# Layer 1 of a four-layer graph network as one written list of 1,056 steps

## The chip, the cores and the metric

The kernel runs on one core of one Trainium2 chip, as one launch that computes all four layers. The metric is the time of an execution on the device in microseconds (us); lower is better. A core has a matrix engine (TensorE, PE in the profile, with its weight loads shown as PEld), three engines for elementwise work (VectorE = DVE, ScalarE = ACT, GpSimd = POOL), and a queue (SyncE, SP) from which most transfers are issued. Each engine takes its own instructions in its own order and waits on semaphores for the others.

## The reference

The data are `x` of 8 batches x 2,048 nodes x 64 features and a normalised adjacency `adj` of 2,048 x 2,048. Every layer ends in `x = layernorm(x + layer(x))`. Layer 0 is a Chebyshev graph convolution with weights for each node, layer 2 a plain graph convolution, layer 3 a graph convolution with symmetric normalisation. Layer 1, where the change is, attends over 64 hyperedges:

```python
h = x @ W
s = leaky_relu(h @ a_node, 0.2)
alpha = softmax(where(H.T > 0, s, NEG), axis=-1)      # over nodes, per hyperedge
agg = einsum('ben,bnf->bef', alpha, h)
beta = sigmoid((h @ a_gn)[:, None, :] + (agg @ a_ge)[:, :, None])
all_he = elu(beta * h + (1 - beta) * agg)             # per hyperedge and node
industry = einsum('nm,bmf->bnf', adj / deg, x @ W_ind)
he = elu(agg)
attn_scores = lambda f: tanh(f @ fcW + fcb) @ av
coefs1 = softmax(where(H > 0, attn_scores(he), NEG))  # over hyperedges, per node
g = einsum('bne,benf->bnf', coefs1, all_he)
pair = stack([industry, g], axis=2)
coefs2 = softmax(attn_scores(pair), axis=-1)
out = einsum('bnk,bnkf->bnf', coefs2, pair)
```

Layer 2 then needs, for every node, `x @ weight_neighbor` (to be multiplied by the adjacency) and `x @ weight_self`.

## The kernel before

The 2,048 nodes are 16 tiles of 128 nodes (`NT = 16`, `P = 128`); a tile's features for all batches are 512 columns (`BC`). Products with the adjacency are done with a 0/1 mask and a scale for each node, on operands split into a high and a low part (`y_hi`, `y_lo`), so that one tile of such a product is 16 x 2 matmuls of 128x512 that accumulate in one PSUM tile. In the profile they appear as `ind` (industry of layer 1) and `a` (layers 2 and 3); the pool `ps_acc` that they accumulate in has a single buffer, so the first product of a tile waits for the scaled copy (`ind`, on ACT, line 658) of the tile before. The mask of a tile is 1 MB, fetched by SP as `mj_l` (two buffers) or, for tiles 0 and 1 of layer 1, in four parts kept in other tiles' homes (`mp_l`, `mp_l1b`).

For every tile j, layer 1 does three things.

- **unit** (`units`, from line 776): `sx` (scores by matmul), `ST` and `tau` (ACT), `gates` (DVE); then, in two halves i = 0, 1 of at most four hyperedges of a node: `ch` (POOL, gate times h), `gp` (PE, gather), `m` and `z` (DVE), `exp` (ACT), `e` (DVE), `w` (POOL); `dp` (PE) and `t3` (ACT) for nodes with more; `a0`, `ga` (POOL sums), `red` (PE), `g` (DVE).
- **product** (`industry`, from line 646): step `i` is a part of the 32 matmuls of industry, step `ind` the scaled copy.
- **mixer** (`mix_and_norm`, from line 917): `dlt` (DVE, industry minus g), `xg` (the kept x is fetched by SP, POOL adds g), `tr`, `sT`, `fc` twice (transpose on PE, copy on ACT, matmul on PE, once for g and once for industry), `th0`, `th1` (ACT, tanh), `sub` (DVE), `df` (PE, line 960: the scores, with `av` repeated in 32 columns and the four blocks in the four column groups of the PE array), `rw` (ACT), `rt` (PE), `sw` (ACT), `mult`, `r`, `s`, `centre` (DVE), `sq` (ACT), `var` (DVE), `rstd` (POOL, two instructions), `x2` (ACT, eight instructions).

`gp` and `exp` use the PSUM pool `ps_g` (one buffer), `fc` the pool `ps_fc` (one buffer), `sx` and `df` the pool `ps_s` (one buffer), and `dp`, `red` and all transposes the pool `ps_m` (two buffers).

The order is written out by hand. Inside `program_order()` (line 213) every instruction of PE, DVE, ACT and POOL is tied to the one before it on its engine, so that the order of the calls is the order on each engine. First comes a head (lines 682 to 757) for the hyperedges' own scores: `agg`, `he`, a transpose, `fche`, the tanh `the`, the scores `sep` (line 723: eight products with one column each), `ese`, then the sums `dnp` for all 16 tiles (line 737). In it six of the 16 steps of tile 1's product are done. Then come the string `ramp` (tiles 0 and 1), the string `turns`, repeated for t = 1 to 14, where turn t works on the unit of tile t + 1 (its `sx` on t + 2), the product of tile t + 1, the mixer's first part of tile t - 1, its second part of tile t - 2 and its end of tile t - 3; and four strings `ending`. A tile's product is eight steps `i` of four matmuls in a turn.

Layer 2's own projections (`features2`, `layer2`, lines 1009 to 1039: a transpose `tr` and the copy `xT`, sixteen small matmuls `u`, then `y_hi` on ACT and two DVE instructions) stand in the strings `ending` as `K` and `L`, that is, after turn 14; K takes its PSUM from `ps_fc`, L from `ps_g`. The first tile of layer 2's product is the step `A` there, two matmuls each. After the list, POOL adds layer 2's bias to the 16 tiles `x2` (line 1127), and layers 2 and 3 run as loops over tiles (from line 1894); their first fetched mask, `mj_l` of tile 1, uses memory that layer 1 gives up.

Of the kernel before, what the change touches and what calls it, by code (L numbers as in the profile page):

```python
# [9 lines left out]
F32 = mybir.dt.float32  # L10
# [53 lines left out]
def kernel(  # L64
# [547 lines left out]
    def layer1(  # L612
# [25 lines left out]
        homes = {"g": (0, 1, 2, 3), "dlt": (4, 5, 7), "ind": (14, 15), "r": (8, 9, 10),  # L638
# [7 lines left out]
        def industry(j):  # L646

            if j == 0:
                acc = early[1]
            else:  # L650
                a = second if j == 1 else mask_tile(mjp, j, "l1")
                acc = ps_acc.tile([P, BC], F32, tag="acc", name=f"ind_{j}")
                for mt in range(NT):
                    times_mask(acc, a, i_hi, i_lo, mt)
                    if mt % 2 == 1 or j == 1:
                        yield "i"
            ind = row("ind", f"ind_{j}")
            nc.scalar.activation(ind, acc, AF.Copy, scale=cols_of["sdeg"][:, j:j + 1])
            ind_of[j] = ind
            yield "ind"  # L660

        g_of, ind_of, dlt_of = {}, {}, {}
        product = {j: industry(j) for j in range(NT)}
        second = mask_parts(own, 1, (7, 8, 9, 12), "l1b")

        def ahead(n):
            for _ in range(n):
                assert next(product[1]) == "i"

        with tc.tile_pool(name="fa", bufs=2) as fa:  # L670
# [10 lines left out]
            with program_order():  # L681
                agg = fa.tile([P, BC], F32, tag="hs", name="agg", bufs=3)
                nc.vector.tensor_tensor(b_view(agg), b_view(aggp), bcast(rden), ALU.mult)

                he = fa.tile([P, BC], F32, tag="xT", name="he")
                nc.scalar.activation(he, agg, AF.Exp, bias=minus1)
                low = slice(64, P)

# [5 lines left out]
                nc.vector.scalar_tensor_tensor(he, he, 1.0, agg, op0=ALU.min, op1=ALU.max)  # L694
                sums = fa.tile([P, 2, B], F32, tag="sums", name="sums", bufs=1)
                late = [own.tile([P, NT - NE, 2, B], F32, tag="b0_11", name="rest_sums")]
                early[0](NT)
                assert next(product[0]) == "ind"
                tr = ps_tr.tile([P, NP, P], F32, tag="tr", name="trhe")
                for pr in range(NP):  # L700
                    transpose(tr[:, pr, :], he[:, pr * P:(pr + 1) * P])
                heT = fa.tile([P, NP * P], F32, tag="hs", name="heT", bufs=3)
                nc.scalar.copy(heT, tr.rearrange("p r c -> p (r c)"))
                parts(agg1, agg)
                ahead(1)
                fc = ps_mm.tile([P, 2, QW], F32, tag="mm", name="fche")
                for h in range(2):
                    rs = slice(h * 64, (h + 1) * 64)
                    nc.tensor.matmul(fc[:, h, :], fcw_sb[rs], heT[rs], start=True, stop=True)
                th = fa.tile([P, 2, QW], F32, tag="the", name="the", bufs=1)  # L710
                nc.scalar.activation(th, fc, AF.Tanh, bias=fcg_sb)
                nc.vector.scalar_tensor_tensor(
                    b_view(he), b_view(agg), -1.0,
                    vecs[:, 2, :].unsqueeze(1).to_broadcast([P, B, C]), op0=ALU.add, op1=ALU.mult,
                )
                nc.vector.tensor_reduce(sums[:, 0, :], b_view(he), AX.X, ALU.add)
                full = fa.tile([P, BC], F32, tag="full", name="full", bufs=1)
                nc.vector.tensor_scalar(full, agg, -1.0, None, op0=ALU.mult)
                parts(nagg, full)
                ahead(3)  # L720
                sp = ps_tr.tile([P, QW], F32, tag="sm", name="sep")
                for b in range(B):
                    nc.tensor.matmul(
                        sp[:, b:b + 1], th[:, b % 2, (b // 2) * P:(b // 2 + 1) * P], av_sb,
                        start=True, stop=True,
                    )
                ahead(2)
                ese = fa.tile([P, B], F32, tag="ese", name="ese", bufs=1)
                nc.vector.tensor_scalar(ese, sp[:, 0:B], TOP, None, op0=ALU.min)
                nc.scalar.activation(ese, ese, AF.Exp)  # L730
                ese2 = fa.tile([P, 2, B], F32, tag="ese2", name="ese2", bufs=1)
                nc.vector.tensor_copy(r_(ese2[:, 0, :]), ese)
                nc.vector.tensor_tensor(r_(ese2[:, 1, :]), ese, ese2[:, 0, :], ALU.subtract)

                def weight_sums(dn, lo, hi):
                    for j in range(lo, hi):
                        nc.tensor.matmul(
                            dn[:, j - lo].rearrange("p k b -> p (k b)"),
                            r_(pT[0:E, j * P:(j + 1) * P]),
                            r_(ese2[0:E].rearrange("p k b -> p (k b)")), start=True, stop=True,  # L740
                        )
# [5 lines left out]

                dn = ps_tr.tile([P, NT, 2, B], F32, tag="tr", name="dnp")
                weight_sums(dn, 0, NE)
                nc.vector.tensor_copy(sums[:, 1, :], ese)  # L750
                parts(ext, sums)
                rec = fa.tile([P, NE, B], F32, tag="rec", name="rec", bufs=1)
                nc.scalar.copy(rec, dn[:, 0:NE, 0, :])
                reciprocals(rec, dn[:, 0:NE, 1, :], 0, NE)
                dn2 = ps_mm.tile([P, NT - NE, 2, B], F32, tag="mm", name="dnp2")
                weight_sums(dn2, NE, NT)
                nc.scalar.copy(late[0], dn2)
# [5 lines left out]
        mjp = stack.enter_context(tc.tile_pool(name="mj1", bufs=2))  # L763
# [153 lines left out]
        def mix_and_norm(j):  # L917

            ind, g = ind_of[j], g_of[j]
            dlt = row("dlt", f"dlt_{j}")
            nc.vector.tensor_tensor(dlt, ind, g, ALU.subtract)
            yield "dlt"
            xr = row("xr", f"xr_{j}")
            nc.sync.dma_start(xr, kept[j])
            r = row("r", f"r1_{j}")
            nc.gpsimd.tensor_tensor(r, g, xr, ALU.add)
            yield "xg"  # L930

            th = wts.tile([P, 2, BC], F32, tag="pm", name=f"th_{j}")
            fcs = []
            for i, src in enumerate((g, ind)):
                mv = ps_m.tile([P, BC], F32, tag="m", name=f"trm_{j}_{i}")
                for pr in range(NP):
                    pc = slice(pr * P, (pr + 1) * P)
                    transpose(mv[:, pc], src[:, pc])
                yield f"tr{i}"
                sT = small("sT", f"sT_{j}_{i}", (P, BC))  # L940
                nc.scalar.copy(sT, mv)
                yield f"sT{i}"
                if i == 1:
                    nc.scalar.activation(th, fcs[0], AF.Tanh, bias=fcg_sb)
                    yield "th0"
                fc = ps_fc.tile([P, 2, BC], F32, tag="fc", name=f"fc_{j}_{i}")
                for h in range(2):
                    rs = slice(h * 64, (h + 1) * 64)
                    nc.tensor.matmul(fc[:, h, :], fcw_sb[rs], sT[rs], start=True, stop=True)  # L949
                fcs.append(fc)  # L950
                yield f"fc{i}"
            nc.scalar.activation(fc, fc, AF.Tanh, bias=fcb_sb)
            yield "th1"
            nc.vector.tensor_tensor(th, fc, th, ALU.subtract)
            yield "sub"
            df = ps_s.tile([P, QW], F32, tag="sm", name=f"df_{j}")
            for half in range(2):
                for h in range(2):
                    k = 2 * half + h
                    nc.tensor.matmul(  # L960
                        df[32 * k:32 * k + 32, 0:2 * P], av32,
                        th[:, h, half * 2 * P:(half + 1) * 2 * P],
                        start=True, stop=True, tile_position=(0, 32 * k),
                    )
            yield "df"
            rows = small("rows", f"rows_{j}", (P, 2 * P), 1)
            nc.scalar.activation(rows, df[:, 0:2 * P], AF.Tanh, scale=0.5)
            yield "rw"
# [48 lines left out]
        def layer2(j):  # L1017
# [21 lines left out]
            )  # L1039

        unit = {j: units(j, g_of) for j in range(NT)}
# [1483 lines left out]
```

## Time and profile before

| | us |
|---|---|
| median of 3 runs | 1240.49 |
| lowest, highest | 1237.93, 1248.48 |
| profiled execution, time | 1245.25 |
| profiled execution, span | 1243.8 |
| start of the first `sx` of tile 0 | 676.42 |
| start of turn 2, of turn 14 (its first `gp`) | 718.09, 903.52 |
| first product of layer 2's tile 1 | 980.11 |

The profile is of one execution, 1.45 us of whose time lie outside its span. It gives the busy time of each engine, the span in 40 slices of 31 us with the granted clock of TensorE in tenths of full speed (9 stands for 0.9 and more), the chain of work that ended last, and groups of instructions by line, with the shape of their operands, their count, busy time and mean. A stretch can be asked for by its times: then the answer holds busy time of each engine, the clock as a fraction, and the share of the DMA engines. "x8" after a group means eight instructions. A matmul's busy time includes its drain, so that successive matmuls overlap: 32 of them at 0.39 us each take 7.4 us.

### The profile page before, as it was taken

To read this page: it belongs to the slowest core of one execution; us is meant where nothing else is said; L and a number is where in the kernel's file an instruction comes from. 1 tells how busy PE (TensorE), PEld (TensorE's weight loads), DVE (VectorE), ACT (ScalarE), POOL (GpSimd) and SP (SyncE) were. 2 spreads that over 40 slices of the span, in tenths; PEclk is the share of its full clock that TensorE was granted. 3 is DMA by queue.
4 is the path that set the end of the run, shared out by engine and by line. 5 is a ranking of instruction groups with operands and counts; after the bars stand their busy time and mean duration, and the time that the engine had idled before them with its cause. 6 is when DMAs were issued, how large, how long until landed. Compare 5 with 4: busy or idle time off the path is not lost.

```text
span 1243.8 us, 19792 instructions
## 1 busy us (share of the span) xinstructions
PE 1201.1 (97%) x7476; PEld 960.9 (77%) x7476; DVE 886.8 (71%) x1670; ACT 391.3 (31%) x1019; POOL 506.6 (41%) x429
## 2 busy tenths in 40 slices
PE   9999899999999999999999899999988999999996
PEld 7877688888888888888887566666656788888885
DVE  4556578888888888888785778888865656565454
ACT  3100102222222222222233567777765411111111
POOL 2000572555555555555312778888861700000000
PEclk9999999999999999999998799999997999999998
DMA  8987833333333333332454222222200333334551
GB/s 291 240 242 202 202 112 111 106 113 106 108 109 113 107 108 106 107 111 94 161 163 152 76 102 102 102 102 94 93 26 1 136 105 133 107 130 161 178 174 66
DMA packets 101416, 157.11 MB, mean 126 GB/s; under 512 B 12992, under 2 KB 64320, under 8 KB 95552
## 3 DMA queue, kind: packets, MB, share of 16 engines
q1 hardware_dynamic: 96512, 151.38, 37.6%
q10 hardware_dynamic: 4368, 4.33, 1.0%
q8 instruction: 61, 1.00, 0.3%
q0 software_dynamic: 432, 0.05, 0.1%
q14 instruction: 43, 0.35, 0.1%
HBM read 117.97 MB, written 37.76 MB: 125 GB/s over the span
## 4 chain that ended last, share of the span: by engine, by line
PE 87%; DVE 4%; DMA 3%; ACT 3%; issue 2%; POOL 1%; SPq 0%; DVEq 0%; ACTq 0%; POOLq 0%
PE pp L1321 26%; PE a L1782 18%; PE ind L1782 9%; PE y2p L1278 9%; PE y1p L569 6%; PE fc L949 3%; DMA adj<-in_at 2%; PE yp L1881 1%; PE gp L851 1%; PE trm L168 1%; PE try L168 1%; PE dp L869 1%; PE hp L1446 1%; PE u L1027 1%; PE red L900 1%
## 5 line engine op out<-in xcount | busy, mean ns | idle before, releaser
L1332 DVE SCALAR_TENSOR_TENSOR r<-pp,emb_sb,r 128x256 f32<-128x256 f32 x512 | 247.4, 483 | 79.0 <-PE pp L1321 64.9
L1321 PE MATMUL pp<-w_sb,y2T 64*128 64x256 f32 x1024 | 154.2, 378 | 3.3 <-DVE y2T L1294 3.3
L1321 PE MATMUL pp<-w_sb,xT 64*128 64x256 f32 x1024 | 155.9, 381 | 0.6 <-DVE r L1332 0.6
L1321 PE MATMUL pp<-w_sb,y1T 64*128 64x256 f32 x1024 | 153.8, 377 | 0.0
L1190 POOL TENSOR_TENSOR ms<-msk,srow 128x1024 f32<-128x1024 f32 x30 | 76.6, 2552 | 95.3 <-DVE msk L449 95.3
L1321 PEld LDWEIGHTS pp<-w_sb,y2T 64*128 64x128 f32 x1024 | 99.8, 188 | 15.0 <-DVE y2T L1294 3.7
L1321 PEld LDWEIGHTS pp<-w_sb,y1T 64*128 64x128 f32 x1024 | 99.6, 188 | 11.4
L1321 PEld LDWEIGHTS pp<-w_sb,xT 64*128 64x128 f32 x1024 | 95.5, 187 | 13.1 <-issue 2.8
L569 PE MATMUL y1p<-x_hi,m 128*128 128x512 f32 x256 | 102.9, 402 | 0.0
L569 PE MATMUL y1p<-x_lo,m 128*128 128x512 f32 x256 | 100.5, 393 | 0.0
L1782 PE MATMUL a<-v_hi,mj_l 128*128 128x512 f32 x256 | 100.1, 392 | 0.0
L1782 PE MATMUL a<-v_lo,mj_l 128*128 128x512 f32 x256 | 100.0, 391 | 0.0
L1782 PE MATMUL a<-y_hi,mj_l 128*128 128x512 f32 x240 | 96.0, 400 | 2.1 <-DMA mj_l<-mask 2.1
L1782 PE MATMUL a<-y_lo,mj_l 128*128 128x512 f32 x240 | 95.9, 400 | 0.0
L1782 PE MATMUL ind<-y_hi,mj_l 128*128 128x512 f32 x224 | 95.4, 426 | 0.0
L1278 PE MATMUL y2p<-y_hi,msk 128*128 128x512 f32 x240 | 94.7, 395 | 0.0
L1278 PE MATMUL y2p<-y_lo,msk 128*128 128x512 f32 x240 | 93.5, 390 | 0.0
L1782 PE MATMUL ind<-y_lo,mj_l 128*128 128x512 f32 x224 | 88.4, 395 | 0.0
L886 POOL TENSOR_TENSOR ez<-ez,coef 128x1024 f32<-128x1024 f32 x32 | 69.8, 2183 | 37.9 <-DVE ez L881 37.9
L1230 DVE SCALAR_TENSOR_TENSOR ms<-ms,adj 128x1024 f32<-128x1024 f32 x30 | 67.2, 2242 | 0.0
L1513 POOL TENSOR_TENSOR hs<-h,es 128x512 f32<-128x512 f32 x15 | 15.6, 1043 | 116.2 <-ACT hgr L1485 116.2
L1782 PEld LDWEIGHTS ind<-y_hi,mj_l 128*128 128x128 f32 x224 | 42.2, 188 | 20.8 <-issue 12.8
(332 smaller groups left out, 2431.9 us busy)
## 6 DMA issues: line engine op xcount, KB each, us to landing
mj_l<-mask SPq DMA_DIRECT2D x45, 1024.0 KB, 4.9
adj<-in_at SPq DMA_DIRECT2D x64, 256.0 KB, 3.8
mask<-msk SPq DMA_DIRECT2D x32, 512.0 KB, 4.5
raw<-in_at SPq DMA_DIRECT2D x31, 512.0 KB, 5.9
oh<-oh SPq DMA_DIRECT2D x32, 128.0 KB, 3.7
xT<-in_xt SPq DMA_DIRECT2D x16, 256.0 KB, 3.2
xs<-in_xn SPq DMA_DIRECT2D x16, 256.0 KB, 2.7
kept<-x SPq DMA_DIRECT2D x16, 256.0 KB, 3.6
```

Source lines behind the costliest of these rows:

```text
L168: nc.tensor.matmul(dst, src, ident, start=True, stop=True, is_transpose=True)
L569: nc.tensor.matmul(accs[q][jj], r_(m[:, t, jj * P:(jj + 1) * P]), r_(part[:, mt, :]), start=i + h + t == 0 and part is x_hi, stop=i == 3 a ...
L851: nc.tensor.matmul(gp[:, u, :], r_(t["oh"][:, 2 * i + u, :]), r_(agg1), start=True, stop=True)
L886: nc.gpsimd.tensor_tensor(by_b(ezs[i]), by_b(ezs[i]), per_b(t["coef"], 2 * i, 2), ALU.mult)
L949: nc.tensor.matmul(fc[:, h, :], fcw_sb[rs], sT[rs], start=True, stop=True)
L1190: nc.gpsimd.tensor_tensor(ms, m, srow[j].unsqueeze(1).to_broadcast([P, 8, P]), ALU.mult)
L1230: nc.vector.scalar_tensor_tensor(ms, ms, 1.0, raws[j][h], op0=ALU.mult, op1=ALU.not_equal, accum_out=bad[:, 2 * j + h:2 * j + h + 1],)
L1278: nc.tensor.matmul(acc, r_(msk[j, mt // 8][:, mt % 8, :]), r_(part[:, mt, :]), start=mt == 0 and part is y_hi, stop=mt == NT - 1 and part ...
L1321: nc.tensor.matmul(pp[:, h, pl, :], terms[j][name][rs, 2 * bq + pl], w_sb[rs, k, dq * 4 * C:(dq + 1) * 4 * C], start=k == 0, stop=k == K - 1,)
L1332: nc.vector.scalar_tensor_tensor(rb, ppv[:, :, dd, :], emb_sb[:, j, d:d + 1], rb, op0=ALU.mult, op1=ALU.add)
L1513: nc.gpsimd.tensor_tensor(b_view(hs), b_view(h_sb[:, j, :]), bcast(es[:, j, :]), ALU.mult)
L1782: nc.tensor.matmul(acc, r_(a[:, mt, :]), r_(part[:, mt, :]), start=mt == 0 and part is hi, stop=mt == NT - 1 and part is lo,)
```

## The change

The change rewrites layer 1's order.

- Every step of a tile becomes a function that can be called alone (`industry`, `units`, `mixer`, `layer2`), and one list of tokens "tile.step" says the order: 33 tokens in the head, 1,023 behind it. `perform` calls them one by one. The strings `ramp`, `turns` and `ending` are gone.
- The steps are no longer in turns. Typically the unit of tile j runs with the product of tile j or j - 1 and the mixers of tiles j - 2 and j - 3. Step `i` is always four matmuls, and the 115 of them behind the head stand one at a time between other steps. Five stand in the head (ten of tile 1's sixteen pairs, six before).
- The masks of tiles 1 to 4 are asked for at the start of layer 1: 1 and 2 in four parts each in homes of other tiles, 3 and 4 in the pool `mj1`, which is opened earlier. From tile 5 on a mask is asked for when the product two tiles before has ended (before: likewise, with the pool opened after the head). The loads of `pT` stand behind these masks on SP and wait for memory of layer 0's last tile; before, they stood ahead of it.
- `xr` of tiles 0 and 1 is fetched at the start of the list and that of tile j + 2 at `xg` of tile j.
- Layer 2's projections are six steps (`f`, `xT`, `mm`, `hi`, `add`, `lo` are their tokens), which begin right after the last product of layer 1 and stand between the steps of tiles 14 and 15. `mm` alternates between `ps_g` and `ps_fc`, except where tile 15's `fc` holds the latter. The sixteen steps `A` stand among them from tile 5's `lo` on.
- The hyperedges' scores `sep` take the form of `df`: four products with `av32` as weights in column groups, a copy of 128x256 by DVE, two transposes, and a view of the result (before: eight products with the tanh as weights and `av` as the only column).
- `dlt` is a `scalar_tensor_tensor` instead of a `tensor_tensor`. Industry has a third home (11).

```diff
-        homes = {"g": (0, 1, 2, 3), "dlt": (4, 5, 7), "ind": (14, 15), "r": (8, 9, 10),
+        homes = {"g": (0, 1, 2, 3), "dlt": (4, 5, 7), "ind": (14, 15, 11), "r": (8, 9, 10),
...
-        second = mask_parts(own, 1, (7, 8, 9, 12), "l1b")
...
+            def products():
+                if j == 0:
+                    early[0](NT)
+                    acc_of[j] = early[1]
+                    return
...
+                for mt in range(done_of[j], done_of[j] + 2):
+                    times_mask(acc_of[j], mask_of[j], i_hi, i_lo, mt)
+                done_of[j] += 2
...
+        at_home = {1: (7, 8, 9, 12), 2: (2, 3, 5, 10)}
+        mjp = stack.enter_context(tc.tile_pool(name="mj1", bufs=2))
...
+        def by_columns(dst, th):
+            for half in range(2):
+                for h in range(2):
+                    k = 2 * half + h
+                    nc.tensor.matmul(
+                        dst[32 * k:32 * k + 32, 0:2 * P], av32,
+                        th[:, h, half * 2 * P:(half + 1) * 2 * P],
+                        start=True, stop=True, tile_position=(0, 32 * k),
+                    )
...
+        head = (
+            "1.mask 2.mask 3.mask 4.mask c.agg 0.i c.hexp c.he 0.ind c.trhe c.agg1 c.heT "
+            "c.fche c.sums c.the c.nagg 1.i c.sep 1.i c.serow c.sert 1.i c.ese c.eexp c.ese2 "
+            "c.dnp c.ext 1.i c.rec c.hgr c.dnp2 1.i c.late "
+        )
...
-                for b in range(B):
-                    nc.tensor.matmul(
-                        sp[:, b:b + 1], th[:, b % 2, (b // 2) * P:(b // 2 + 1) * P], av_sb,
-                        start=True, stop=True,
-                    )
...
-            nc.vector.tensor_tensor(dlt, ind, g, ALU.subtract)
...
+                nc.vector.scalar_tensor_tensor(
+                    t["dlt"], ind_of[j], 1.0, g_of[j], op0=ALU.mult, op1=ALU.subtract
+                )
...
+                    "0.xr 1.xr c.rests 0.sx 0.dp 0.ST 0.gates 0.gp0 0.tau 1.sx 0.ch0 0.m0 0.gp1 1.ST "
+                    "1.dp 1.gates 0.m1 0.ch1 1.tau 2.sx 0.z0 1.i 1.ch0 0.t3 2.gates 1.i 0.exp0 0.z1 "
+                    "1.i 2.tau 0.e0 0.exp1 1.gp0 1.ch1 2.ST 0.e1 1.ind 2.i 0.w0 1.t3 1.m0 1.gp1 2.i "
+                    "1.z0 0.w1 2.i 0.a0 1.exp0 2.i 1.m1 0.ga 1.e0 0.red 3.sx 1.z1 2.ch0 2.gp0 3.ST "
+                    "2.dp 0.g 1.exp1 2.m0 1.w0 0.tr0 2.i 0.sT0 1.e1 0.tr1 2.i 2.z0 0.xg 2.xr 0.sT1 "
+                    "0.fc0 0.dlt 2.exp0 1.a0 3.gates 2.i 0.th0 1.w1 2.e0 2.i 3.tau 0.fc1 2.ind 2.ch1 "
+                    "2.gp1 0.th1 3.i 2.m1 2.w0 2.t3 0.sub 1.red 4.sx 1.ga 2.z1 3.dp 4.ST 4.gates 2.a0 "
...
+                    "9.i 8.sT1 8.dlt 11.tau 7.df 10.gp0 8.th0 9.w1 9.i 10.m0 7.rw 8.fc1 6.x2 10.z0 "
+                    "7.rt 10.ch1 9.i 10.exp0 9.ga 9.red 9.i 10.t3 10.e0 9.i 9.g 11.ch0 8.th1 10.gp1 "
+                    "9.i 7.sw 10.m1 10.w0 7.mult 12.sx 10.z1 9.i 11.mask 12.ST 9.tr0 7.r 9.ind 9.xg "
...
+                    "15.dlt 0.mm/g 1.xT 15.th0 2.f 0.add 3.f 0.hi 1.mm/f 2.xT 0.lo 4.f 1.hi 1.add "
+                    "2.mm/g 3.xT 1.lo 5.f 2.hi 2.add 3.mm/f 4.xT 2.lo 6.f 3.hi 3.add 4.mm/g 5.xT 3.lo "
+                    "15.tr1 4.hi 4.add 5.mm/f 15.sT1 4.lo 14.rt 5.hi 5.add 7.f 6.xT 0.A 5.lo 14.sw "
+                    "6.mm/g 14.mult 14.r 8.f 6.hi 6.add 15.fc1 7.xT 6.lo 9.f 14.s 15.th1 7.mm/g "
+                    "14.centre 8.xT 15.sub 1.A 7.hi 10.f 9.xT 2.A 7.add 14.sq 15.df 7.lo 8.mm/f 15.rw "
...
+                    "10.mm/f 11.xT 15.r 14.x2 9.lo 12.f 13.f 15.s 3.A 9.add 10.hi 4.A 15.centre "
+                    "11.mm/g 12.xT 10.lo 15.sq 10.add 14.f 11.hi 5.A 15.var 13.xT 12.mm/f 11.lo "
+                    "15.rstd 11.add 6.A 12.hi 12.add 13.mm/g 14.xT 12.lo 15.x2 7.A 13.add 14.mm/f 8.A "
+                    "13.hi 14.add 15.f 14.hi 13.lo 9.A 15.xT 14.lo 10.A 15.mm/g 11.A 15.hi 15.add "
+                    "12.A 15.lo 13.A 14.A 15.A "
```

## The prediction

> **What bounds the kernel now.** I read the slices first, then the chain of waits with its shares, then the chain in order of time through layer 1, then busy times by stretch.
>
> ```profile
> PE   9999899999999999999999899999988999999996
> PEclk9999999999999999999998799999997999999998
> PE 87%; DVE 4%; DMA 3%; ACT 3%; issue 2%; POOL 1%; SPq 0%; DVEq 0%; ACTq 0%; POOLq 0%
> ```
>
> PE bounds nearly everything: 87% of the chain. Its weak slices are 22 to 23 and 30 to 31, the start and the end of layer 1. Three stretches, first the ramp (tile 0's `sx` to turn 2), then one turn, then the end:
>
> ```profile
> 676.42:718.09 41.67, 37.10 (x130) 25.05 (x131) 28.20 (x50) 19.21 (x52) 29.55 (x19) 0.76 0.25 89
> 718.09:733.54 15.45, 15.45 (x76) 10.16 (x75) 12.88 (x20) 9.45 (x22) 10.74 (x8) 1.00 0.28 102
> 918.90:980.11 61.21, 49.30 (x408) 35.84 (x407) 35.51 (x55) 35.11 (x81) 21.14 (x19) 0.89 0.08 28
> ```
>
> Columns: stretch and length, busy time of PE, PEld, DVE, ACT, POOL, granted clock, DMA share, GB/s. In a turn PE is busy throughout at clock 1.00; nothing is to be had there. In the ramp and the end it is idle, and the clock is at 0.76 and 0.89. So the change can gain where PE waits, and lose wherever it makes PE wait in the 13 full turns.
>
> The price of each step on PE comes from the chain in one turn (start, length, group):
>
> ```profile
> 731.47 2.07 PE ind L1782 x8
> 733.54 0.46 PE gp L851 x2
> ...
> 735.47 1.06 PE fc L949 x4
> 736.53 0.59 PE trm L168 x4
> 737.12 0.86 PE dp L869 x2
> ...
> 744.57 0.86 PE red L900 x2
> 745.42 0.93 PE ind L1782 x4
> 746.35 0.57 PE df L960 x8
> ```
>
> So `i` (four matmuls) costs 0.93, `gp` 0.46 and 0.66, `fc` 1.06, `red` 0.86, `dp` 0.86 + 0.23, `tr` 0.44 and 0.59, `sx` 0.81, `rt` 0.22, and `df` 0.57 and 0.21 more that the products behind it lose (2.07 for eight, elsewhere in the turn 1.86). Of the end, at clock 1.00: `f` 0.58, `mm` 1.10 (16 matmuls `u`), `A` 0.46. On the others, from the groups by form: DVE 1.22 for the 1,024-column steps `m0`, `z`, `e`, `sub`, 0.70 for `m1`, 0.68 for 512 columns, 0.81 for `gates`; ACT 1.12 for `exp`, `th`, 1.75 for `t3`, 2.03 for `x2`, about 0.6 for 512 columns; POOL 1.91 and 1.04 for `ch`, 2.2 for `w`, 1.29 for `a0`, `ga`, `xg`, 1.92 for `rstd`. A tile's sums are PE 15.5, DVE 13.6, POOL 13.1, ACT 12.2.
>
> **What the list's work costs.** PE's price of the 1,023 steps behind the head is 269.7 (7.8 + 0.2 per tile for unit and mixer, 115 `i`, and 16 times `f`, `mm`, `A`: 34.3). The same work lay between 676.42 and 980.11, that is 303.7, with 1.9 more (two `i` now stand in the head). 32 us are lost in ramp and end.
>
> **Head.** Up to `fche` (667.22) nothing moves. Then PE: `sep` took 1.68 and is now priced like `df`, 0.57; added are DVE's copy of 128x256 (nearest rows: 0.39 for ACT's `rows`, half of 0.68 for a DVE copy of 512: 0.35) and two transposes (0.22). An `i` stands after each, so the longer chain from the tanh's end (669.58) runs: `sep` 670.2, copy 670.7, `rt` behind an `i` 671.4, `ese`, exponential and split (0.75 in the trace) 672.3; four `dnp`, `i`, twelve `dnp`, `i`. The sixteen took 3.31, which I leave. First `sx`: 677.0 instead of 676.42, bounds 676 and 678, with 1.9 more done. On SP `pT` now stands behind masks 1 to 4 and, by the waits in the built program, needs the memory of layer 0's last tile, free after the last `aggp` (663.1), where it went out at 629.4; by the row of `pT` (7.0 us to landing) and eight issues of 0.44 its last piece is there at about 673, where the last `dnp` needs it at 675: hidden, worth up to 2 us if not. `oh` of tile 0 follows at 667 and lands 4.6 later, before 677. 3 MB of masks land under layer 0's last tile; the early part of mask 0 queues behind one of them (4.9), from 632 to 640, and is needed at 646.
>
> **Ramp.** I walked the list with those durations from 677.0, giving each step the later of its engine's turn and its operands. PE does 5.73 of `sx`, `dp`, `gp` of tiles 0 to 2 and three `i` while tile 0 goes `gates`, `tau`, `ch0`, `z0`, `exp0`, `e0`; the second `gp0` needs `e0` (`ps_g` has one buffer) and waits 1.6. The first product of tile 2 needs `ind` of tile 1, which stands on ACT behind `exp1` and `ST`: 0.6. POOL has most work in the next stretch (16.9 against PE's 15.1) but started ahead. Tile 3's first product comes at 703.8: 24.1 of price and 2.7 idle. Before, 26.8 of price took 41.67. Clock: in the trace it fell to 0.50 during the sixteen `dnp`, after a stretch (664 to 666) with PE busy for 0.52 of 2 us and then matmuls of 1 and 16 columns; here 512-column products stand among them, and I price at full clock. At 0.76, as before, the ramp costs 7 more.
>
> **Middle and end.** From there to the last `A` PE's price is 245.6. Summed from one tile's first product to the next one's, PE is the largest everywhere but in two sections (tile 7: DVE 18.8 against 17.8; tile 12: 13.7 against 13.4): +1.4. What remains is waiting inside a section. Below: 0, as in 13 turns. Above: 18, what the end lost before. In one loop that I followed (tiles 9 and 10), `gp1` waits for `gp0`, `m0`, `z0`, `exp0`, `e0`: 4.8 plus semaphores 0.3, against 5.9 of PE work between; `fc1` has 0.5 to spare. Margins are of the size of one small step, so some are missed: 0.6 per tile, 8, nearer to the turns' row because every resource is the turns'. In the end, two buffers for `mm` give 1.10 + 0.59 + 0.69 + 0.69 and 0.2 of semaphores, 3.3 for two tiles, just under PE's 3.4; before, one buffer at a time left PE waiting for `y_lo`:
>
> ```profile
> 928.58 0.69 DVE x L1036
> 929.27 0.60 DVE y_lo L1037
> ...
> 975.22 4.76 DMA mj_l<-mask
> ```
>
> Tile 15's chain from `df` to `f` is 9.8 against 13.0 of PE work in between. The last line is layer 2's next mask, waited for 2.3 us by PE. It now waits for tile 15's `rstd`, behind which `x2`, `f`, `xT`, `mm`, `hi`, `lo`, `A` still take 6.3: hidden; 4.9 if these are quicker. Uninterrupted products also spare layer 2's first 4 us at clock 0.5 to 0.6: 1.2.
>
> **Sum.** 703.8 + 245.6 + 1.4 + 8 = 958.8 instead of 980.11, and 1.2: **-22.5 us**. Against the profiled execution (span 1243.8, time 1245.25) that is 1222.7; it lies 4.8 above the median, so against 1240.49 I predict 1218.0. Without waits 1208.6; with 18 of them 1228.
>
> `dlt` as `scalar_tensor_tensor`: 0.684 for both forms in the turns. But one `dlt` took 1.66, while POOL's sum ran, whose successor then took 1.72 instead of 1.29:
>
> ```profile
> 703.34 1.66 DVE L924 TENSOR_TENSOR dlt<-ind,g 128x512 f32<-128x512 f32 x1
> ```
>
> The `scalar_tensor_tensor` rows with two operands in SBUF never exceed 0.69, POOL's `w` beside them goes from 1.90 to 2.28. I take 0 on DVE, and 2.2 for `w` holds the rest. The Trainium skill, "SBUF — State Buffer", section "Who interferes with whom", says that a VectorE instruction with two SBUF inputs and a GpSimd one that reads SBUF exclude each other for a whole instruction. It speaks against the change, which gives up turns where they rarely meet: were four such steps of each tile blocked by 1 us, DVE would need 17.6 of 15.5 and the sum be +11 instead of -22.5. The trace has one such wait in 16 `dlt`, so I weigh it low.
>
> **Rivals.**
> - *The margins are missed*: the list is in order on every engine, so one late step (a POOL sum, `ind` behind `exp` on ACT) delays the next. DVE at 88% and POOL at 85% of a tile speak for it, their idle 2 us per turn against. At 2.3 per tile instead of 0.6 the gain is gone: 1236 to 1245.
> - *The clock*, slower than before: between 922 and 934 PE was busy for 7.86 of 12 us and was then granted 0.50 until 938; `u` took 2.01 instead of 1.09. The old turns held 1.00 by running products of 8 and 12; single `i` between waiting steps may not. Half clock for a time T costs T/2. It decides once PE idles by a third, 5 us in a tile: from 70 us of it on (4 or 5 tiles) the result is slower by over 1%, 1253 to 1265. The skill's "TensorE: Matmul & The Clock Gate", section "A second HAM failure mode: psum-queue depth-cycling", describes such small pauses; the turns' 1.00 stands against it.
> - *The change does only half of what it says*: layer 2's projections in the gaps lengthen tiles 14 and 15 (`fc` shares `ps_fc` with `mm`), and the end loses its 18 as before: 1228.
>
> **Chances.** Forecast 0.60 (1208 to 1225), half 0.10 (1225 to 1231), margins missed 0.17 (1228 to 1250), clock 0.13. A measurement of this kernel tells 1% from nothing: faster by over 1% 0.68, within 1% 0.19, slower 0.13. The range goes from 1206 (no waits, a quicker head) to 1242, with the slowest cases outside.
>
> **What would show it.** First `sx` near 677; tile 3's first product near 704 at clock near 1.0; some 15.5 per tile; layer 2's tile 1 at 957 to 962 with no wait for a mask; layers 2 and 3 unchanged in length. Sections longer than PE's price with idle named by DVE or POOL prove the first rival, clock under 0.9 between 704 and 950 the second.

## The result, and the profile after

The changed kernel takes **1228.35 us** (median of 4 executions, 1225.07 to 1229.4), the kernel before, run beside it, 1242.3 (4, 1237.93 to 1248.48): a ratio of **0.988, interval 0.983 to 0.993**. In a second comparison it was 1230.92 (10 executions) against 1239.97 (17), ratio 0.993, interval 0.991 to 0.996; one more execution of the kernel before ran at a mean granted clock of 0.84 instead of 0.98, took 1354.88 and is not counted. So the changed kernel is faster, by some 9 to 14 us and not by the 22.5 forecast.

The profiled execution has a span of 1227.7 and a time of 1229.4; its span is 16.1 shorter than that of before. The slices and the chain's shares of the page, after:

```profile
PE   9999899999999999999999999999999999999996
...
PEclk9999999999999999999998999999999999999998
...
PE 73%; DVE 13%; DMA 4%; issue 3%; ACT 3%; POOL 2%; SPq 0%; DVEq 0%; ACTq 0%; POOLq 0%
```

Both weak spots of PE's row (slices 22 to 23, 30 to 31) are filled, and the clock is granted in full but for slice 22 and the last. Yet PE holds 73% of the chain where it held 87%, and DVE 13% instead of 4%: TensorE shows as busy nearly everywhere, but what sets the end has moved in part to VectorE. The busy times by stretch (columns as in the prediction) tell where. In order: the ramp, one section of the middle (from tile 10's first product to tile 11's), the end (last product of layer 1 to the first of layer 2's tile 1), and all that follows:

```profile
677.59:703.33 25.74, 24.27 (x113) 16.40 (x112) 22.52 (x43) 15.81 (x43) 20.11 (x13) 1.00 0.14 41
...
832.14:848.77 16.63, 14.28 (x70) 9.15 (x67) 15.46 (x29) 10.78 (x31) 11.36 (x8) 1.00 0.24 86
927.90:966.41 38.51, 38.43 (x379) 29.40 (x378) 28.31 (x44) 26.53 (x59) 11.70 (x11) 1.00 0.18 70
966.41:1227.70 261.29, 251.31 (x1185) 205.16 (x1183) 148.58 (x240) 40.60 (x81) 13.39 (x10) 0.99 0.38 131
```

Ramp and end are as hoped: PE busy for 24.3 of 25.7 and 38.4 of 38.5, clock 1.00. The middle isn't: PE works 14.3 of 16.6 in that section, DVE 15.5. The list's DVE work there is 13.7 by the prices of the prediction, and `gates` of one more tile, 0.8, fell into it. The rest is steps that took longer than their price, and four groups say which (smallest, median and largest duration in ns):

```profile
L1008 DVE SCALAR_TENSOR_TENSOR dlt<-ind,g x16: 672/729/2146, 699.0 to 929.0; 128x512 f32<-128x512 f32 x16
L1071 DVE SCALAR_TENSOR_TENSOR dlt<-sw,dlt x16: 677/688/2442, 710.5 to 950.8; 128x512 f32<-128x512 f32 x16
L1076 DVE SCALAR_TENSOR_TENSOR r<-dlt,r x16: 674/691/2277, 713.8 to 951.6; 128x512 f32<-128x512 f32 x16
L1086 DVE SCALAR_TENSOR_TENSOR r<-s,r x16: 678/1374/2082, 716.2 to 954.0; 128x512 f32<-128x512 f32 x16
```

These are `dlt`, `mult`, `r` and `centre`. The same four in the kernel before:

```profile
L924 DVE TENSOR_TENSOR dlt<-ind,g x16: 679/684/1662, 703.3 to 941.6; 128x512 f32<-128x512 f32 x16
L979 DVE SCALAR_TENSOR_TENSOR dlt<-sw,dlt x16: 680/684/685, 721.7 to 962.0; 128x512 f32<-128x512 f32 x16
L983 DVE SCALAR_TENSOR_TENSOR r<-dlt,r x16: 679/681/693, 723.5 to 962.8; 128x512 f32<-128x512 f32 x16
L988 DVE SCALAR_TENSOR_TENSOR r<-s,r x16: 679/681/693, 730.9 to 966.4; 128x512 f32<-128x512 f32 x16
```

There none but `dlt` exceeded 0.693. Summed over the 64 instructions, what goes beyond each line's fastest is 4.8, 7.7, 7.4 and 10.8: **30.7 us** (before: 1.4, 0.1, 0.1, 0.1). Apart from one step of tile 0 (`a0`), they alone of DVE's large steps here have both operands in SBUF; `z`, `e`, `sub` and `g`, which read one from PSUM, stay within 3% of their shortest.

The timeline (start, duration, engine, line, operation; rows of VectorE and GpSimd alone) shows a collision in the changed kernel:

```profile
891.85 0.68 DVE L1071 SCALAR_TENSOR_TENSOR dlt<-sw,dlt 128x512 f32<-128x512 f32 x1
892.08 2.22 POOL L971 TENSOR_TENSOR ez<-ez,coef 128x1024 f32<-128x1024 f32 x1 [0.35 <-DVE ez L966]
892.57 2.28 DVE L1076 SCALAR_TENSOR_TENSOR r<-dlt,r 128x512 f32<-128x512 f32 x1
894.26 2.35 POOL L925 TENSOR_TENSOR d<-h,sig 128x1024 f32<-128x1024 f32 x1
```

GpSimd's `w` starts while `mult` runs and is lengthened from 1.90 to 2.22. Then `r` starts while `w` has 1.73 left and takes 2.28, which is 0.68 and 1.60 more: it waits until `w` is nearly over. The next GpSimd step, `ch`, starts inside `r` and is lengthened in turn. Over the 57 instructions of these lines between 700 and 932, the excess is the rest of the GpSimd step under way less 0.13 in nearly every case (the longest, 2.44, came when a step had 0.04 left and then waited for the whole of the next one). The exception is GpSimd's `rstd` (the power of 128x8): DVE steps that started beside it took 0.68 to 0.69. That is how the old turns escaped, as the timeline of the kernel before shows:

```profile
735.88 1.67 POOL L1000 TENSOR_TENSOR rstd<-var,mhalf 128x8 f32<-128x8 f32 x1
736.51 0.69 DVE L924 TENSOR_TENSOR dlt<-ind,g 128x512 f32<-128x512 f32 x1
...
737.11 0.69 DVE L979 SCALAR_TENSOR_TENSOR dlt<-sw,dlt 128x512 f32<-128x512 f32 x1
...
746.33 0.68 DVE L988 SCALAR_TENSOR_TENSOR r<-s,r 128x512 f32<-128x512 f32 x1
746.50 2.28 POOL L886 TENSOR_TENSOR ez<-ez,coef 128x1024 f32<-128x1024 f32 x1 [0.64 <-DVE ez L881]
```

`dlt` and `mult` stand beside `rstd`, and `r` and `centre` start about 0.2 ahead of a `w`, so that GpSimd waits and not VectorE. Thirteen turns had this same layout; in the list it comes only now and then.

### The profile page after: what moved, and what is told of

It reads as the page before. It is cut to its first block, busy times and chain, and to the rows that moved or that the text cites. A ratio compares the mean times of both kernels' runs of the same rounds, so it can differ in the third digit from the quotient of the medians.

```text
span 1227.7 us, 19772 instructions
## 1 busy us (share of the span) xinstructions
PE 1187.7 (97%) x7470; PEld 942.0 (77%) x7470; DVE 911.2 (74%) x1671; ACT 388.8 (32%) x1019; POOL 512.4 (42%) x429
## 3 DMA queue, kind: packets, MB, share of 16 engines
q1 hardware_dynamic: 96944, 151.38, 38.4%
## 4 chain that ended last, share of the span: by engine, by line
PE 73%; DVE 13%; DMA 4%; issue 3%; ACT 3%; POOL 2%; SPq 0%; DVEq 0%; ACTq 0%; POOLq 0%
PE pp L1457 26%; PE a L1918 19%; PE y2p L1414 9%; PE y1p L569 5%; PE ind L1918 3%; DMA xraw<-in_xn 2%; DVE d L947 2%; DVE ez L966 1%; DVE gp L944 1%; PE u L1146 1%; DMA adj<-in_at 1%; PE yp L2017 1%; PE try L168 1%; DVE r L1086 1%; PE hp L1582 1%
## 5 line engine op out<-in xcount | busy, mean ns | idle before, releaser
L1918 PE MATMUL ind<-y_hi,mj_l 128*128 128x512 f32 x208 | 91.2, 438 | 0.1
L1918 PE MATMUL ind<-y_lo,mj_l 128*128 128x512 f32 x208 | 81.9, 394 | 0.0
L971 POOL TENSOR_TENSOR ez<-ez,coef 128x1024 f32<-128x1024 f32 x32 | 65.2, 2039 | 12.8 <-DVE ez L966 12.7
L925 POOL TENSOR_TENSOR d<-h,sig 128x1024 f32<-128x1024 f32 (+1 forms) x32 | 50.1, 1569 | 32.6 <-ACT sig L903 18.3
```

The source lines that it names most:

```text
L925: nc.gpsimd.tensor_tensor(d[:, 0:n].rearrange("p u (b c) -> p u b c", b=B), b_view(h_sb[:, j, :]).unsqueeze(1).to_broadcast([P, n, B, C]), ...
L971: nc.gpsimd.tensor_tensor(by_b(ezs[i]), by_b(ezs[i]), per_b(t["coef"], 2 * i, 2), ALU.mult)
L1918: nc.tensor.matmul(acc, r_(a[:, mt, :]), r_(part[:, mt, :]), start=mt == 0 and part is hi, stop=mt == NT - 1 and part is lo,)
```

## The experiments

Two theories. **Collisions**: these four steps and GpSimd's steps hold each other up, DVE is late for TensorE's next operand, and this is the missing gain. **Order**: the list's margins are missed anyhow, and the long DVE steps fill idle time. A third, named in the first expectation, is that other traffic slows these steps. "The stretch" is that from tile 3's first product to layer 2's tile 1: 703.33 to 966.41 in the changed kernel, 263.1 (263.2 in its second profile).

### Four steps with one operand in SBUF

```diff
-                nc.vector.scalar_tensor_tensor(
-                    t["dlt"], ind_of[j], 1.0, g_of[j], op0=ALU.mult, op1=ALU.subtract
-                )
+                nc.vector.tensor_reduce(t["dlt"][:, 0:B], b_view(ind_of[j]), AX.X, ALU.add)
...
-                nc.vector.scalar_tensor_tensor(
-                    t["r"], t["dlt"], 0.5, t["r"], op0=ALU.mult, op1=ALU.add
-                )
+                nc.vector.tensor_reduce(t["dlt"][:, 0:B], b_view(t["r"]), AX.X, ALU.add)
```

and likewise `mult` (a sum over `sw`) and `centre` (a sum over `s`). Such a kernel computes something else; it is run for its time alone.

> Leaves out the arithmetic of four VectorE steps of each tile of layer 1 (dlt, mult, r, centre): each becomes a sum over 512 columns with one operand in SBUF, in the same place and behind the same waits, of the same length (the sums s and var take 0.67 to 0.69 in every profile here). The output is therefore not the layer's. Theory 'collisions' (a VectorE step with two operands in SBUF and a GpSimd step hold each other up, which cost these four lines 30.7 us beyond their 0.68 in the changed kernel): all 64 take 0.66 to 0.70, VectorE's busy time between the first sx and layer 2's tile 1 falls from 278 to 246 to 250, the stretch from tile 3's first product to layer 2's tile 1 falls from 263.1 to 250 to 255, the time by 8 to 13 against the changed kernel's 1228. Rival 'order' (the list's margins are missed whatever VectorE does): the lines shorten, but the stretch stays at 260 to 264 and the time within 3 of 1228. Rival 'other traffic' (the long steps are slowed by TensorE, ScalarE or transfers): the sums are stretched as well, up to 2 us.

It took 1206.99 (ratio to the kernel before 0.977, interval 0.971 to 0.982). All four lines were at 0.67 to 0.69, so no other traffic slows them:

```profile
L1008 DVE TENSOR_REDUCE dlt<-ind x16: 673/677/690, 695.7 to 906.8; 128x8 f32<-128x512 f32 x16
L1068 DVE TENSOR_REDUCE dlt<-sw x16: 674/677/687, 707.3 to 928.5; 128x8 f32<-128x512 f32 x16
L1071 DVE TENSOR_REDUCE dlt<-r x16: 674/685/687, 709.0 to 929.3; 128x8 f32<-128x512 f32 x16
L1078 DVE TENSOR_REDUCE r<-s x16: 675/680/686, 711.5 to 931.7; 128x8 f32<-128x512 f32 x16
```

The stretch fell to 944.11 - 700.09 = **244.0**, by 19.1, more than the 8 to 13 expected. Between first `sx` and layer 2's tile 1 DVE's busy time is 224.8 instead of 254.3 (these are the rows by stretch, which count overlapping instructions once; with each counted in full it is 274 and 245, not the 278 and 246 to 250 of the expectation). PE's idle is gone, here in the section of tile 10 again, in the one after it, and in the end:

```profile
832.66:847.84 15.18, 15.18 (x76) 9.56 (x75) 11.31 (x13) 11.15 (x28) 13.06 (x10) 1.00 0.23 82
818.86:832.66 13.80, 13.80 (x70) 9.49 (x68) 12.34 (x22) 10.41 (x32) 9.07 (x8) 1.00 0.35 121
905.60:944.11 38.51, 38.45 (x378) 29.46 (x377) 28.27 (x44) 26.21 (x58) 11.69 (x11) 1.00 0.18 69
```

Tile 10's section is 13.80, all of it TensorE, instead of 16.63. The end is 38.51 in both kernels: all 19.1 came from the middle. With the collisions away TensorE is idle for 0.06 us of the whole stretch, where it was for 13.8 in the changed kernel; "order" has nothing left to explain.

### The same edit in the kernel before

> The kernel before, with the same four steps (dlt, mult, r, centre) turned into sums with one operand in SBUF; their arithmetic is left out. Theory 'collisions': the old turns had hardly any (1.4 us in all, dlt and mult beside rstd, r and centre started just ahead of a GpSimd step that waited for them), so nothing is to be had: the turns stay at 15.45 and the time within 0.5% of the kernel before, where the same edit took 21 us off the changed kernel. GpSimd's w beside r and centre shortens from 2.2 to 1.9. Rival: the sums are cheaper for another reason than the second operand (fewer bytes written, a wait that went with dlt), and the kernel before gains 8 us or more as well.

1241.51 against 1242.46 (10 and 13 executions), ratio 0.9997, interval 0.997 to 1.003. The turns stay at 15.45 (734.65 to 750.09, for example), and `w` in them goes from 2.25 to 1.90 (medians). In the turns a cheaper VectorE step could not show, since TensorE is busy throughout. But the ramp and the end, where TensorE waits, gain nothing either: 46.2 from the first `sx` to tile 3's first product with and without the edit, and 257.8 against 257.5 from there to layer 2's tile 1. The edit that takes 19.1 us off the changed kernel's stretch takes nothing off the old one.

### Small operands in PSUM

In this and all that follow, the computation is whole.

```diff
+        bank = ps_s.tile([P, QW], F32, tag="sm", name="bank")
...
-                t["sw"] = small("sw", f"sw_{j}")
+                t["sw"] = bank[:, 464 + 8 * (j % 2):472 + 8 * (j % 2)]
...
-                t["s"] = small("s", f"s_{j}")
+                t["s"] = bank[:, 480 + 8 * (j % 2):488 + 8 * (j % 2)]
```

(`sx` and `df` use other columns of the same bank.)

> Only the small operands sw and s (128x8) of mult and centre are moved from SBUF to PSUM, in the bank of sx and df; the arithmetic is unchanged. Theory 'collisions': mult and centre, which then have one operand in SBUF, take 0.68 in all 32 cases (before this: up to 2.44 and 2.08, 18.4 us too much in all), dlt and r keep their long instances. The time falls by 2 to 7, less if s now waits for the df of the next tile, with which it shares the bank. Rival 'other traffic': mult and centre are still stretched to 2 us. Rival 'order': they shorten and the time stays within 2.

1220.48 (0.986, interval 0.981 to 0.992). Run once more on the chip of the second comparison above:

> The kernel with sw and s in PSUM once more, beside the changed kernel on the same chip: faster by 6 to 9, mult and centre never over 0.7.

**1217.07** beside the changed kernel's 1230.92, which is 13.9 less where 6 to 9 were expected; the ratios to the kernel before are 0.982 (0.976 to 0.989) and 0.993 (0.991 to 0.996). The stretch is 252.0 and 252.2, 11.1 and 11.0 less than the changed kernel's. Most of what the second comparison has beyond these 11 lies between `fche` and tile 3's first product, where the changed kernel's profile holds 10.2 us of half clock and this one none. The lines of `mult`, `r` and `centre` in that second profile:

```profile
L1073 DVE SCALAR_TENSOR_TENSOR dlt<-bank,dlt x16: 678/680/692, 707.9 to 937.2; 128x512 f32<-128x512 f32 x16
L1078 DVE SCALAR_TENSOR_TENSOR r<-dlt,r x16: 679/718/2117, 709.7 to 938.0; 128x512 f32<-128x512 f32 x16
L1088 DVE SCALAR_TENSOR_TENSOR r<-bank,r x16: 673/684/692, 713.1 to 940.4; 128x512 f32<-128x512 f32 x16
```

Operation, shape, place and arithmetic are the same; only where an operand of 128x8 lies differs. `mult` and `centre` no longer meet anything; `r`, with both in SBUF, still does. It is the second SBUF operand that counts, not its size. The shared bank has a price of its own: in the first profile TensorE is idle for 5.9 of the stretch, and 2.3 of that are waits of matmuls that write this bank for `mult` and `centre`, which read it.

### No centre

The mean goes into `x2` as a bias, the variance is corrected by the squared mean; DVE loses a step, ACT and POOL get two small ones each.

```diff
-                r = b_view(t["r"])
-                nc.vector.scalar_tensor_tensor(
-                    r, bcast(t["s"]), -1.0 / C, r, op0=ALU.mult, op1=ALU.add
-                )
+                t["m"], t["m2"] = small("lm", f"lm_{j}"), small("lm2", f"lm2_{j}")
+                nc.scalar.activation(t["m"], t["s"], AF.Copy, scale=-1.0 / C)
+                nc.scalar.activation(t["m2"], t["s"], AF.Square, scale=1.0 / C)
...
-                        x2[:, j, bc], t["r"][:, bc], AF.Copy, scale=t["rstd"][:, b:b + 1]
+                        x2[:, j, bc], t["r"][:, bc], AF.Identity, scale=t["rstd"][:, b:b + 1],
+                        bias=t["m"][:, b:b + 1],
```

> Computes the same normalisation without the step centre: the mean goes into x2 as a bias, and the variance is the mean square less the squared mean. VectorE loses one step per tile (0.68, and 0.67 more of waiting on average, 21.6 us in all); ScalarE gets two steps of 128x8 (about 0.2 each, by the row of ese 0.21), GpSimd two (0.25 each, by the row of var 0.24). Theory 'collisions': what VectorE no longer does comes off the stretch in part, since VectorE set the pace in about half of the sections: 263.1 becomes 256 to 260, the time falls by 3 to 7. The three other lines keep their long instances. Rival 'order': no gain, and 0 to 4 more, since ScalarE and GpSimd have more to do.

1224.48 (0.989, 0.984 to 0.995); stretch 260.5, just outside the expected 256 to 260. DVE's busy time fell by 18.1 (254.3 to 236.2), about as much as with `sw` and `s` in PSUM (236.7), but the stretch only by 2.6 instead of 11: between tile 3 and layer 2 TensorE now waited 2.4 on ScalarE's `sT` (0.8 in the changed kernel) and 3.8 on `e` (2.3). A smaller total of DVE doesn't make a late step early. With `sw` in PSUM as well:

> Both edits at once: the mean as a bias of x2 (no step centre) and sw in PSUM (mult has one operand in SBUF). Of the four lines only dlt and r can still meet a GpSimd step. Theory 'collisions': VectorE is freed of 16 x 0.68 more than with sw and s in PSUM, but ScalarE and GpSimd have 0.4 and 0.5 per tile more; the stretch from tile 3's first product to layer 2's tile 1 (252.0 there, 260.5 without centre alone, 244.0 with four sums) becomes 249 to 254, the time 1217 to 1222. If the small steps on ScalarE and GpSimd cost more than the centre, it lands above 254.

1221.27 (0.986, 0.983 to 0.990), stretch 255.6, just above the expected range. But this profile holds 3.4 us of half clock from 908.6 on, behind a wait of TensorE of 2.1; that is worth up to 1.7, so the range was perhaps met. That the small steps on ScalarE and GpSimd cost more than `centre` with its operand in PSUM (252.0) fits, by 2 to 4 us in one profile.

### Layer 2's projections behind everything else

The 112 steps of layer 2 moved to the end of the list, in their own order.

> Layer 2's projections and its tile 0 (112 steps) stand behind all other steps of layer 1, in their own order. By the prediction's step for the end, TensorE's 37 us of them no longer cover the chains of tiles 14 and 15: from the last product's end to tile 15's x2 TensorE waits for most of 9.8 (tile 15 from df on) and of what stands before it (fc, tanh, sub, some 5): the stretch from tile 15's first product to layer 2's tile 1, 50.95 in the changed kernel, becomes 61 to 67 and the time rises by 10 to 16. Rival 'the end was worth nothing' (the 16 projections go through as fast at the end, the gain came from ramp and clock): within 4.

1247.81 (1.008, interval 1.005 to 1.011): without this part the change would be **slower** than the kernel before. The section from tile 15's first product to layer 2's tile 1 is 69.1 instead of 50.95, 18.1 more, above the expected 10 to 16. This row of it shows both losses:

```profile
930.00:943.90 13.90, 3.48 (x18) 2.20 (x18) 6.38 (x9) 6.95 (x23) 3.81 (x4) 0.55 0.10 26
```

TensorE is busy for 3.5 of 13.9 while the chains of tiles 14 and 15 run (its longest wait is 7.6, for a copy on ScalarE that stands behind tile 15's `x2`), and the clock falls to 0.55, which the expectation had not priced.

### dlt as it was

```diff
-                nc.vector.scalar_tensor_tensor(
-                    t["dlt"], ind_of[j], 1.0, g_of[j], op0=ALU.mult, op1=ALU.subtract
-                )
+                nc.vector.tensor_tensor(t["dlt"], ind_of[j], g_of[j], ALU.subtract)
```

> Only dlt is again a tensor_tensor, in the changed kernel. Prediction: nothing, since both forms read two operands in SBUF: dlt takes 0.68 where no GpSimd step is under way and up to 2.1 where one is, some 4 to 6 us too much in all 16, time within 4 of 1228. Rival: the tensor_tensor does not meet GpSimd, and dlt takes 0.68 in all 16.

`dlt` is stretched to 2.14 at most and 4.7 us in all, as with the other form. But this one execution took 1238.3, with a stretch of 261.9; the loss stands in layer 2:

```profile
963.89 12.43 POOL L1261 TENSOR_TENSOR x<-x,bias_sb 128x512 f32<-128x512 f32 x10
...
966.14 10.73 DVE L140 SCALAR_TENSOR_TENSOR r<-s_l,r 128x512 f32<-128x512 f32 x1
```

One VectorE step with two operands in SBUF waited through eight of GpSimd's additions of the bias, which follow each other without a gap, and TensorE waited 8.4 for what came of it. Whether this goes with the form was asked of the second comparison:

> The kernel with dlt as tensor_tensor again, which took 1238.3 in one execution: layer 1 was as long as in the changed kernel, but in layer 2 the centre of tile 0 (VectorE, two operands in SBUF) took 10.7 us while eight additions of the bias ran one behind the other on GpSimd, where it takes 0.8 in the others. If that was the luck of one execution, the time is 1226 to 1231 and this step takes 0.8 to 1.5; if the form of dlt or the timing that follows from it fixes it, the time is 1236 to 1240 and the step takes 10 again.

> The changed kernel itself, to stand beside the next three on the same chip: 1225 to 1230, the same long instances of dlt, mult, r and centre (28 to 33 us beyond 0.68 each).

1231.64 (9 executions) and 1230.92 (10): no difference, and that step took 0.87 in both profiles. The form is worth nothing; the 10.7 is a matter of single executions (the next kernel's profile has it too, 10.74).

### Order alone: dlt and r beside rstd

Still with `sw` and `s` in PSUM.

```diff
-8.var 12.ch0 11.gp1 10.dlt 11.i 11.m1 10.tr1 13.tau 11.z1 11.w0 11.i 9.fc1 11.exp1 8.rstd 11.i
+8.var 12.ch0 11.gp1 11.i 11.m1 10.tr1 13.tau 11.z1 11.w0 11.i 9.fc1 11.exp1 8.rstd 10.dlt 11.i
```

(a piece of the list of steps, with one of the seventeen moves as an example)

> sw and s in PSUM, and the order alone changed: six steps rstd are moved to stand right before a step r of another tile, and eleven steps dlt to stand right behind a step rstd, since in the kernel before the dlt and mult that ran beside rstd (GpSimd's power of 128x8, 1.67) took 0.69. Theory: dlt and r, which were 12 us too long in all, lose half of that or more, and the stretch from tile 3's first product to layer 2's tile 1 (252.0) becomes 246 to 250, the time 1214 to 1218 where the kernel without this has 1220. Rival: the engines' places in time drift against the list, dlt and r meet other GpSimd steps as often as before, and the moved steps are late for others: 252 to 258.

1225.6 (1219.85 to 1230.87), stretch 256.9: no gain on the 252 without. `dlt` and `r` did lose a third of their excess (12.0 to 8.0), and tile 4's section went from 20.8 to 19.5. But those of tiles 6, 13 and 14 grew, 18.9, 19.4 and 19.9 where they had been 17.7, 15.9 and 17.6: moved steps came late for others, as the rival said. In tile 13's section one can see it: with `rstd` moved, `x2` started late on ScalarE, the scaled copy `ind` stood behind it, and TensorE waited 2.9 for that copy. Tile 14's growth is another matter: right behind that wait the clock was at half for 6.8 us (886.3 to 893.1), worth up to 3.4. (The profiled execution, 1230.87, also holds the 10.74 above.)

### The head's clock

```diff
-            "1.mask 2.mask 3.mask 4.mask c.agg 0.i c.hexp c.he 0.ind c.trhe c.agg1 c.heT "
+            "1.mask 2.mask 3.mask 4.mask c.agg 0.i c.hexp c.he 0.ind c.trhe 1.i c.agg1 c.heT "
...
-            "c.dnp c.ext 1.i c.rec c.hgr c.dnp2 1.i c.late "
+            "c.dnp c.ext 1.i c.rec c.hgr c.dnp2 c.late "
```

> sw and s in PSUM, and in the head one step i of tile 1 is moved from the end of the head to the place between trhe and fche. Theory 'clock of the head': TensorE was busy for 0.63 of 2 us there and was then granted 0.50 for 6.8 us; with 0.93 us of products in that gap the drop does not come or comes later, fche takes 1.1 instead of 2.1, and from fche to the first sx it takes 10.0 to 11.0 instead of 12.2. The time falls by 1 to 2 against the same kernel without it (1220.5). Rival: TensorE still waits for ScalarE's copy and the clock falls all the same: 12 to 12.5, and no difference.

1218.73 (0.983, 0.980 to 0.986) against 1220.48: inside the uncertainty. From `fche` to the first `sx` it took 9.0, but the half clock only came later: 0.53 between 676 and 688, and the ramp took 30.5 at a mean of 0.78 instead of 25.7. Nor does the unmoved head always have the drop: from `fche` to tile 3's first product it took 35.3 where the clock never fell, 37.9 with 6.8 us of half clock in the head, 39.5 with 10.2 us in the ramp. What decides it was not found.

## Why the prediction was right, and where it was not

The direction and the range held, the place of the gains too; one term was mis-sized by 8 us. The range, up to 1242, holds even no change at all (1240.49), so that it held says little. 1228.35 lies outside the band that was held likeliest (1208 to 1225, 0.60) and in that of the rival "only half" (1225 to 1231, 0.10), whose cause did not occur: that its number came is luck. By the steps:

| step (us) | predicted | profile |
|---|---|---|
| up to `fche` | unchanged | 1.8 shorter |
| `fche` to first `sx` | 9.8 | 12.2 (9.5 to 12.2 in others) |
| first `sx` to tile 3's first product | 26.8 | 25.7 |
| from there to layer 2's tile 1 | 255.0 | **263.1** |
| from there to the end of the span | 262.5 | 261.3 |
| span against before | -22.5 | -16.1 |

- **Up to fche** nothing was changed that matters: the 1.8 arises at 150 us, where the clock was 0.57 for 4 us in the one execution and 1.00 in the other.
- **Head.** The terms were right; half clock, at another place than before, made it 12.2 in this profile. The walk's 36.6 from `fche` to tile 3's first product lies within the 35.3 to 40.7 of all profiles that have this head. No wait for `pT` or a mask shows.
- **Ramp.** 25.7 wherever the clock stayed at 1.00, against 26.8 walked.
- **Middle and end: here the step failed.** "Margins are of the size of one small step, so some are missed: 0.6 per tile, 8" was the size of small delays between engines in order. The stretch lost 17.5 over PE's 245.6, not 9.4, and the margins were not the cause: with the four lines at 0.68 it is 244.0, PE's price to 1%. The price list was right and the waits for order alone were nothing; the whole loss is VectorE against GpSimd.
- **dlt and the collisions.** "I take 0 on DVE" is right for the form. But the paragraph saw the collision in one row, 1.66, and weighed it by its frequency before: one in 16 (a second `dlt`, at 918.23, took 1.01 and was overlooked). The frequency was that of the old layout, which the change gives up, as the same paragraph said. Price per tile: 30.7 / 16 = 1.9, against the 4 it had reckoned for all four steps blocked. The rule of the Trainium skill, "SBUF — State Buffer", section "Who interferes with whom", that it set against this row, was the better guide, and the runs agree with it: two SBUF inputs met GpSimd and one did not (`mult` up to 2.44 against 0.69), and the wait lasted for the rest of the instruction less 0.13. They do not agree throughout: GpSimd's `rstd` also reads SBUF and held nobody up, 0.68 to 0.69 beside it.
- **The end.** 38.4 of 38.5 busy, and no mask waited for (2.1 before): as reckoned with two PSUM buffers for `mm`, which no run tested by themselves. The version with the projections last shows what this part is worth: 18.1 us in its section, more than the whole gain. Behind layer 2's tile 1 the forecast 1.2 came, 1.25 up to its tile 15; 1.1 more lie in the last 10 us of the span, and why is open.
- **Rivals.** "Margins missed" came true by half (1.35 us per tile over 13, where 2.3 would have taken all) by a mechanism that its wording did not name. "Clock" did not come in this kernel: 1.00 in every section from 703 to layer 2, with 13.8 us of idle in pieces of 1.3 at most. So it doesn't show the small pauses of the Trainium skill's "TensorE: Matmul & The Clock Gate", section "A second HAM failure mode: psum-queue depth-cycling", at work in the middle. What did halve the clock there in three variants came behind one longer wait each: 2.1 (no centre, `sw` in PSUM), 2.9 (order alone) and 3.0 (projections last); a wait of 2.1 in "no centre" alone did not halve it. (In the kernel before, the spell that the rival cites ran from 932.2 to 939.1, so it began within the stretch given.) "Only half" did not come either: the end lost nothing.

## What to carry to other kernels

Before steps are moved against each other on VectorE and GpSimd, list those VectorE steps that read two operands from SBUF: each may cost the rest of a GpSimd step, and a regular loop may hide them all without saying so. A collision that is rare in the profile of before is priced by the layout to come, not by its count. Putting one operand in PSUM, be it 128x8, takes the step out of it: that took 11 us off the stretch (14 off the time, 1217.07 against 1230.92, in part by the clock). What is left is 252 against 244.0, mostly `dlt` and `r`, and some 2 us of waits for the shared bank; an operand of `dlt` and `r` in PSUM wasn't tried.

## What the hardware showed beyond what was expected

- A VectorE step that lost to GpSimd can lose again: it took 10.7 us through eight GpSimd steps without a gap (in two profiles), where it slipped in between two of them in 0.83 to 0.93 in nine others. It started 0.32 before the end of a GpSimd step in both and 0.28 to 0.38 before it in the nine; what decides was not found.
- GpSimd's `rstd`, 1.67 us on 128x8, let VectorE's steps pass at 0.68 to 0.69, its sums and products of 512 or 1,024 columns did not. Long and busy isn't the same as in the way.
- Spells at half clock come in steps: by the trace's record of the clock those around the head lasted 3.4, 6.8, 10.2 or 13.7 us, at different places with the same program (6.8 from 665.1 in the one profile of the changed kernel, 10.2 from 672.7 in the other), and cost up to 5.4 us (35.3 without one, 40.7 with two, 3.4 and 10.2 long).
